# Four transformer layers on one NeuronCore: experts ordered by hand in steps of one, and sigmoid attention run inside the feed-forward's steps

## The chip, the cores and the metric

The program runs on one core of one Trainium2 chip. The core has a matrix engine (TensorE, "PE"; its weight loads are listed as "PEld"), VectorE ("DVE"), ScalarE ("ACT"), GpSimd ("POOL") and a DMA queue that SyncE ("SP") feeds. The engines run side by side, each through its own list of instructions in order, and wait for each other by semaphores. The metric is device time in microseconds; less is better.

## What is computed

A tensor x (32 x 64 x 256, here 2048 tokens of 256 values) goes through four layers of cross-attention to a context of the same shape and a feed-forward. The kernel calls the eight parts A to H. The change touches four of them:

```python
# D: causal attention with 16 heads, then four experts, two per token
a = attention(layernorm(x));  h = x_n + a                 # x_n: layernorm of x
t = layernorm(h)
raw = softmax(t @ w_gate);  top_vals, top_idx = top_k(raw, 2)
comb = scatter(softmax(top_vals), top_idx)                # (token, expert)
hmid = gelu(t @ we1[e] + be1[e]);  eout = hmid @ we2[e] + be2[e]
x = x + h + sum_e comb[:, e] * eout
# E: local attention (only its preparation is touched)
# F: two ternary products, silu(first) * second, an RMS norm, rounding, a third ternary product
x = x + linear3(silu(linear1(x_n)) * linear2(x_n))
# G: sigmoid attention of a sequence's 64 tokens; its channels play the part of positions
s = sigmoid(einsum('bdn,bdm->bnm', x_n, ctx) / 8)
x = x + einsum('bvn,bnm->bvm', ctx, s)
# H: shared and routed experts
```

## The kernel before, in words

The tokens lie in 16 tiles of 128 (xs), the context likewise (cs), and both stay in SBUF for the whole program. A stage opens pools of SBUF and PSUM tiles. Stages lie on the left and the right side of SBUF in turn, and memory of a closed pool can be used by a later one only after the last instructions on it. A stage's weights are loaded at the start of the stage before (load_D to load_H). Where no order is forced, a scheduler orders instructions for each engine; inside `tc.manual_schedule()` they stand as the program issues them. Pieces that are to lie among another stage's work are generators: each `next` issues the instructions up to the next `yield`.

**D, attention** (run_D_attention): 64 units of one head for four tiles, three units deep; a unit's steps are projections (L926, L928 to L935), scores (L941 to L953), transposes (L960), products (L970), and the sum over heads into hs (output, L985, L986).

**D, experts** (run_D_moe): four groups of four tiles. For each group in turn: norm_T normalises (ln_stats L82 to L87, ln_apply L91, transposes L97, gain and shift L521), the gate product gpl (L1038), softmax_small (L132 to L140), top2 (L115 to L127), the weights comb (to L1053) and comb's transpose (L1057). Then for each expert: hidden products hmp (L1065) with Gelu (L1068), and for each tile the output product ep (L1072), accumulated with its weight into hs on VectorE (L1075). Biases (L1079, L1080) and the sum into xs (L1081) end the group. After each expert one `next` goes to one of two generators: ternary (weights of F are read, scaled and rounded to tern, L1210 to L1226), or first_of_E (operand buffers of E are filled on VectorE, L153, and its first two tiles prepared). The scheduler orders all this.

**F** (run_F), in a hand-made order: in step t each part works on the tile t - lag. VectorE has summed (L1380), hidden (L1329), second_norm (L1348), first_sizes (xk L1284, am L1286, L1272, the factor sca L1275), second_rounding (amb L1355, hq L1358) and deviations (L1261 to L1266). ScalarE has first_copy (xT), second_copy (hT), gates (sl, Silu), squares (junk) and first_rounding (xq). GpSimd has the powers rr (L1350) and s (L1268) and gained (xr L1344). PE has the transposes xqT and hqT and the products l (L1314) and op (L1376). [...]xqT one bank, l four, hqT two, op one.

**G** (run_G), after F, groups of four tiles: normalise (L82 to L91), transpose the context (gcT L97, copied to cT on VectorE, L1409), for each of a tile's two sequences the products sp (L1415) and Sigmoid (L1419), the product gop (L1425), and the sum into xs (L1428). It lies on the left side; the weights of H (L1439 to L1447), H's table owner (L1460 to L1464) and its pools lie on the right, where F's pools lay.

**H** (run_H): routing of a group (hgp L1478), then 14 chunks of pgate and pup products (L1523), Silu (L1531), products on VectorE (L1533, L1535) and hout (L1502).

Of the kernel before, what the change touches and what calls it, by code (L numbers as in the profile page):

```python
# [17 lines left out]
P = 128  # L18
T = 2048
D = 256  # L20
# [11 lines left out]
def tile_net(ctx: ExitStack, tc: tile.TileContext, a: dict, out: bass.AP):  # L32
# [115 lines left out]
    def operand_buffers(pool, k, b):  # L148

        pair = {}  # L150
        for kind, value in (("k", 1.0), ("q", 0.0)):
            pair[kind] = pool.tile([P, 16, D], BF, name=f"st{kind}{b}")
            V.memset(pair[kind][64:P], value)  # L153
        k.setdefault("st", []).append(pair)
# [699 lines left out]
    def run_D(w, side):  # L854
        with tc.tile_pool(name="Dh", bufs=1, side=side) as hpool:
# [3 lines left out]
            hs = [hpool.tile([P, D], F32, name=f"h{i}") for i in range(NT)]  # L859
            run_D_attention(w, side, hs)  # L860
            run_D_moe(w, side, hs)

    def run_D_attention(w, side, hs):
# [4 lines left out]
        with ExitStack() as es:  # L868
# [4 lines left out]
            hnT = [tpool.tile([P, 2, 512], F32, name=f"hnT{g}") for g in range(NG)]  # L873
# [113 lines left out]

            weights_of(0)
# [19 lines left out]

    def run_D_moe(w, side, hs):
        with tc.tile_pool(name="DM2", bufs=1, side=side) as wpool, tc.tile_pool(  # L1010
            name="DMw", bufs=2, side=side
        ) as pool, tc.tile_pool(
            name="DMp", bufs=2, space=PSUM
        ) as psum:
# [4 lines left out]
            next(tern, None)  # L1019

            def others():
                for _ in range(5):
                    for gen in (first, tern):
                        next(gen, None)
                        yield
                while True:
                    for _ in range(4):
                        next(first, None)
                    yield

            other = others()
            for g in range(NG):
                ids = range(4 * g, 4 * g + 4)
                hT = norm_T(pool, psum, ids, src=hs, wb=(w["ln2_w"], w["ln2_b"]))
                gp = psum.tile([P, 4, 4], F32, tag="tp", name="gpl")
                for j in range(4):
                    for c in range(2):
                        PE.matmul(  # L1038
                            gp[:, j, :], hT[:, c, j * P : (j + 1) * P], w["gate"][:, c, :], start=c == 0, stop=c == 1
                        )  # L1040
                raw = softmax_small(pool, gp, 4, 4)
                (s1, s2), (m1, m2) = top2(pool, raw, 4, 4)
                e2 = pool.tile([P, 4], F32, name="e2")
                V.tensor_tensor(e2, m2, m1, ALU.subtract)
                S.activation(e2, e2, AF.Exp)
                w1 = pool.tile([P, 4], F32, name="w1")
                V.tensor_scalar(w1, e2, 1.0, None, ALU.add)
                V.reciprocal(w1, w1)
                V.tensor_tensor(e2, e2, w1, ALU.mult)
                V.tensor_tensor(s1, s1, bc(w1, 2, [P, 4, 4]), ALU.mult)  # L1050
                V.tensor_tensor(s2, s2, bc(e2, 2, [P, 4, 4]), ALU.mult)
                comb = pool.tile([P, 4, 4], F32, name="comb")
                V.tensor_tensor(comb, s1, s2, ALU.add)  # L1053

                tp = psum.tile([P, 4, P], F32, tag="tp", name="dcombT")
# [4 lines left out]
                for e in range(4):  # L1060
                    hm = pool.tile([P, 2, 512], F32, name="hm")
                    for ic in range(2):
                        hp_ = psum.tile([P, 512], F32, name="hmp")
                        for c in range(2):
                            PE.matmul(  # L1065
# [42 lines left out]
    def first_of_E(w, psum):  # L1108
# [4 lines left out]
        for b in range(4):  # L1113
            operand_buffers(cp, w["k"], b)
            yield
# [530 lines left out]
```

## Time and profile before

| what | value |
|---|---|
| median of the runs shown | 2878.74 us (2876.58 to 2881.87, 3 runs) |
| the profiled execution | 2879.53 us |
| its span from first to last instruction | 2877.8 us |
| busy: PE, DVE, ACT, POOL | 2468.2 (86%), 1914.5 (67%), 1531.7 (53%), 1506.4 us (52%) |
| chain that ended last, by engine | PE 50%, DVE 22%, issue 9%, POOL 5%, ACT 2%, DMA 1% |
| attention of D ends | about 1844.4 us |
| first step of F; first instruction of H's gate product | 2347.9; 2559.48 us |

The profile is of one execution. A row of the timeline has start, length, engine, line, operation, out<-in, shape and count; in brackets stands the idle time of the engine before it and what ended that. Rows of a matmul overlap, so a row of eight can be shorter than eight single ones. The chain of what ended last gives at each time the one instruction that the end waited for. A line number can be a helper's: L82 to L91 are the statistics of any stage, so the tile's name says which.

### The profile page before, as it was taken

Reading aid. Unit: us, or ns where it says so; the run is one execution under the profiler, and the core shown is the slowest. Engines: PE = TensorE matmul, PEld = TensorE weight load, DVE = VectorE, ACT = ScalarE, POOL = GpSimd, SP = SyncE. Lnnn points to the kernel's source line nnn. Section 1 sums busy time; section 2 is a strip of 40 time slices with the busy share of each in tenths; the row PEclk is TensorE's granted clock in tenths of the full one; section 3 lists DMA queues with packets and bytes.
Section 4 is the critical chain, followed back from the end, with each engine's and each line's share of the span. In section 5 each row is a group of like instructions: output and inputs, shape, how many; then the busy total and the mean of one; then the engine's idle time right before and its main releaser. Section 6 shows DMA issues by size and latency. Waiting matters only on the chain.

```text
span 2877.8 us, 44432 instructions
## 1 busy us (share of the span) xinstructions
PE 2468.2 (86%) x16072; PEld 1449.1 (50%) x16072; DVE 1914.5 (67%) x3989; ACT 1531.7 (53%) x2145; POOL 1506.4 (52%) x1681
## 2 busy tenths in 40 slices
PE   4989798777778777689999999789888976789999
PEld 2545344344444444346666666556555533445555
DVE  7877554699999999775455455663577669833332
ACT  1657221599999999655555555353345556521110
POOL 4655433588888888665555555311587754400000
PEclk9999899999999999889999999888999988999999
DMA  6553000499999999910000000001443300200000
GB/s 166 128 116 70 23 1 1 106 202 203 202 207 201 204 201 199 186 59 8 15 15 15 8 1 1 30 30 24 103 93 89 92 1 1 76 1 8 8 8 8
DMA packets 610599, 223.70 MB, mean 78 GB/s; under 512 B 547366, under 2 KB 600524, under 8 KB 605772
## 3 DMA queue, kind: packets, MB, share of 16 engines
q1 hardware_dynamic: 607308, 220.07, 35.0%
q8 instruction: 127, 2.08, 0.3%
q10 hardware_dynamic: 3072, 0.79, 0.2%
q14 instruction: 92, 0.75, 0.1%
HBM read 66.91 MB, written 18.87 MB: 30 GB/s over the span
## 4 chain that ended last, share of the span: by engine, by line
PE 50%; DVE 22%; issue 9%; POOL 5%; ACT 2%; DMA 1%; ACTq 0%; DVEq 0%; POOLq 0%; SPq 0%
DVE e L789 11%; PE yp L985 4%; PE ppq L926 3%; PE ppk L926 3%; PE hout L1502 3%; PE vp L914 3%; PE pgate L1523 3%; PE pup L1523 3%; PE sp L944 2%; PE ep L1072 2%; PE op L970 2%; PE hmp L1065 2%; PE sc L759 1%; PE op L495 1%; POOL e L286 1%
## 5 line engine op out<-in xcount | busy, mean ns | idle before, releaser
L813 ACT ACTIVATE ei<-e,nb,sq 128x2048 int16<-128x2048 f32 x256 | 535.4, 2092 | 43.4 <-DVE nb L810 39.7
L823 POOL CAST eb<-ei 128x2048 bf16<-128x2048 int16 x256 | 482.5, 1895 | 116.1 <-ACT ei L813 102.0
L759 PE MATMUL sc<-kT,qz 128*128 128x512 bf16 x1024 | 298.1, 382 | 142.0 <-DVE e L789 139.9
L246 DVE TENSOR_REDUCE negm<-s 128x2 f32<-128x512 f32 (+1 forms) x512 | 300.9, 611 | 130.6 <-PE s L242 127.4
L789 DVE TENSOR_SCALAR_CACHE_REDUCE e<-sc,mx 128x1024 f32<-128x1024 f32 x256 | 326.1, 1274 | 0.8 <-DVE nb L810 0.7
L789 DVE TENSOR_SCALAR_CACHE_REDUCE e<-sc 128x1024 f32<-128x1024 f32 x256 | 312.4, 1220 | 10.5 <-PE sc L759 10.5
L278 ACT ACTIVATE e<-s 128x1024 f32<-128x1024 f32 (+1 forms) x256 | 233.2, 915 | 152.8 <-PE s L274 117.3
L242 PE MATMUL s<-stk,stq 96*128 96x256 bf16 (+1 forms) x1024 | 192.2, 271 | 41.2 <-DMA d3k<-t3k 24.8
L759 PEld LDWEIGHTS <-qz 128*128 128x128 bf16 x1024 | 94.9, 97 | 261.2 <-issue 202.6
L934 POOL TENSOR_TENSOR rwq<-rwq,sin 128x512 f32<-128x512 f32 x64 | 81.1, 1268 | 240.1 <-ACT rwq L931 203.7
L274 PE MATMUL s<-stq,stk 128*128 128x256 bf16 (+1 forms) x1024 | 180.6, 262 | 10.8 <-DMA stq<-nm 5.4
L772 PEld LDWEIGHTS <-vz 128*64 128x64 bf16 x4096 | 123.2, 110 | 114.0 <-issue 113.9
L946 DVE TENSOR_REDUCE mx<-sp 128x4 f32<-128x512 f32 x64 | 44.3, 692 | 192.7 <-PE sp L944 192.7
L772 PE MATMUL av<-eT,vz 128*64 128x128 bf16 x4096 | 164.0, 223 | 7.3 <-DMA eT<-eb 7.2
L87 POOL TENSOR_TENSOR rstd<-ve,mhalf 128x1 f32<-128x1 f32 (+1 forms) x56 | 42.4, 757 | 240.9 <-DVE ve L85 145.9
L931 ACT ACTIVATE rwq<-ppq,dbq 64x512 f32<-64x512 f32 x128 | 87.4, 683 | 148.9 <-DVE rtq L928 148.0
L1533 DVE TENSOR_TENSOR hm<-pup,sl 128x512 f32<-128x512 f32 (+1 forms) x56 | 38.7, 692 | 191.1 <-PE pup L1523 187.4
L242 PEld LDWEIGHTS <-stq 96*128 96x128 bf16 x1024 | 93.6, 101 | 131.9 <-issue 108.6
L296 PE MATMUL o<-e,vmo 128*32 128x256 f32 (+1 forms) x2048 | 151.1, 367 | 7.4 <-POOL e L286 6.0
L1531 ACT ACTIVATE sl<-pgate 128x512 f32<-128x512 f32 (+1 forms) x56 | 33.4, 597 | 219.2 <-PE pgate L1523 219.1
L286 POOL TENSOR_SCALAR_AFFINE_SELECT e<-e 128x256 f32<-128x256 f32 (+1 forms) x256 | 133.2, 547 | 31.0 <-ACT e L278 30.3
L914 PE MATMUL vp<-Dwv,hnT 128*128 128x512 f32 x256 | 123.8, 605 | 4.0 <-ACT hnT L889 4.0
(349 smaller groups left out, 5518.5 us busy)
## 6 DMA issues: line engine op xcount, KB each, us to landing
stk<-d3k SPq DMA_DIRECT2D x96, 192.0 KB
stq<-d3q SPq DMA_DIRECT2D x96, 192.0 KB
d3k<-t3k SPq DMA_DIRECT2D x160, 64.0 KB
d3q<-t3q SPq DMA_DIRECT2D x96, 64.0 KB
eT<-eb SPq DMA_TRANSPOSE x256
fw<-in_L_ffn_w SPq DMA_DIRECT2D x3, 1024.0 KB
x<-in_x SPq DMA_DIRECT2D x16, 128.0 KB
c<-in_ctx SPq DMA_DIRECT2D x16, 128.0 KB
```

The source lines that it names most:

```text
L242: PE.matmul(sc[:, hh, lo:hi], qs[0:96, 2 * hp + hh, qc * P : (qc + 1) * P], ks[0:96, 2 * hp + hh, lo:hi], start=band is None, stop=True, s ...
L246: V.tensor_reduce(negm[:, qc, 2 * hp : 2 * hp + 2], sc[:, :, lo:hi], AX.X, ALU.max, negate=True)
L274: PE.matmul(sc[:, c, lo:hi], ks[:, h, lc * P : (lc + 1) * P], qs[:, h, lo:hi], start=True, stop=True)
L278: S.activation(e[:, :, lo:hi], sc[:, :, lo:hi], AF.Exp, scale=scale)
L759: PE.matmul(sc[:, k0 : k0 + 512], qz[i % 2][:, h, :], kT[:, h // 2, 1024 * part + k0 : 1024 * part + k0 + 512], start=True, stop=True,)
L772: PE.matmul(av[i][r0 : r0 + 64, h // 4, :], vz[:, kt, h // 4, h % 4, :], eT[:, kt, :], start=h == 0 and kt < 2, stop=h == H - 1 and kt >= ...
L789: V.tensor_scalar(e, scs.pop((n, part)), 1.0, mx[:, 0:1] if part else LOWEST, ALU.mult, ALU.max, accum_out=mx[:, part : part + 1],)
L813: S.activation(ei, es_.pop(n), AF.Exp, bias=nb, scale=sq[i][:, h : h + 1], accum_out=sums[i][:, h : h + 1],)
L823: G.tensor_copy(eb, eis.pop(n - 1))
L914: PE.matmul(vp, hnT[g][:, c, j * P : (j + 1) * P], wv[:, c, :], start=c == 0, stop=c == 1)
L926: PE.matmul(pp, wt[:, c, hh * P : (hh + 1) * P], hnT[g][:, c, :], start=c == 0, stop=c == 1)
L1523: PE.matmul(pp[:m], w[nm + "s"][:, c, cols], xnT[:, c, :], start=c == 0, stop=c == 1)
```

## The change

In **D**, routing becomes a generator, routed_D, with seven pieces. The first group's runs in attention's last steps; each later group's runs among the experts of the group before it. run_D_moe is put under manual_schedule, as 16 steps of one expert and one group: the hidden products of step n + 1 are issued ahead of the outputs of step n, and in each step up to two `next` each go to ternary, first_of_E and routing. E's operand buffers are filled on GpSimd (the new last argument). ternary has two more yields.

**F and G** are one loop of 24 steps. G's eight parts are entries of F's table with lags 5 to 7. They use F's banks (xqT, hqT0, hqT1, op); Sigmoid is written as Tanh, with a half of the context's row sums (half) as bias; normalising and the final sum are on GpSimd, the copy of the context on ScalarE. run_G returns at once. In `scales`, the factor (sca and scb) is computed by scalar_tensor_tensor with s as second tensor, not by tensor_scalar.

```diff
-    def operand_buffers(pool, k, b):
+    def operand_buffers(pool, k, b, eng=None):
...
-            V.memset(pair[kind][64:P], value)
+            (eng or V).memset(pair[kind][64:P], value)
...
+    def routed_D(w, hs, g, pool, psum, tag):
+        ids = range(4 * g, 4 * g + 4)
+        mv, rstd = ln_stats(pool, [hs[i] for i in ids])
+        yield
...
+        for j0 in (0, 2):
+            xn = []
+            for j in (j0, j0 + 1):
+                xn.append(pool.tile([P, D], F32, name="hn"))
+                ln_apply(xn[-1], hs[4 * g + j], mv, rstd, j)
+            yield
...
+            for j in range(2):
+                for c in range(2):
+                    PE.transpose(tp[:, c, j, :], xn[j][:, c * P : (c + 1) * P], ident)
+            for c in range(2):
+                S.activation(
...
+        w["routed"][g] = [hT]
+        yield
+        gp = psum.tile([P, 4, 4], F32, tag=tag, name=f"gpl_{g}", bufs=2)
+        for j in range(4):
+            for c in range(2):
+                PE.matmul(gp[:, j, :], hT[:, c, j * P : (j + 1) * P], w["gate"][:, c, :], start=c == 0, stop=c == 1)
...
+        S.activation(raw, raw, AF.Exp)
+        yield
...
+        (s1, s2), (m1, m2) = top2(pool, raw, 4, 4)
...
+        S.activation(e2, e2, AF.Exp)
+        yield
...
+        V.tensor_tensor(comb, s1, s2, ALU.add)
+        w["routed"][g].append(comb)
+        yield
...
+            ahead = routed_D(w, hs, 0, pool, psum, "vy")
...
+                if u >= NU - 3:
+                    next(ahead, None)
+            for _ in ahead:
+                pass
...
+        ) as pool, tc.tile_pool(name="DMp", bufs=2, space=PSUM) as psum, tc.manual_schedule():
...
+            def hidden(n):
+                g, e = divmod(n, 4)
+                hT = w["routed"][g][0]
+                hm = hms[n] = pool.tile([P, 2, 512], F32, name="hm")
+                for ic in range(2):
+                    hp_ = psum.tile([P, 512], F32, name="hmp")
                     for c in range(2):
                         PE.matmul(
+                            hp_, w["we1"][:, c, e, ic * P : (ic + 1) * P], hT[:, c, :], start=c == 0, stop=c == 1
                         )
+                    S.activation(hm[:, ic, :], hp_, AF.Gelu, bias=w["be1"][:, e, ic : ic + 1])
+            def output(n):
+                g, e = divmod(n, 4)
+                _, comb, combT = w["routed"][g]
+                hm = hms.pop(n)
+                for j in range(4):
+                    i = 4 * g + j
+                    ep = psum.tile([P, D], F32, name="ep")
+                    for ic in range(2):
+                        PE.matmul(
+                            ep, hm[:, ic, j * P : (j + 1) * P], w["we2"][:, e, ic, :], start=ic == 0, stop=ic == 1
+                        )
+                    V.scalar_tensor_tensor(hs[i], ep, comb[:, j, e : e + 1], hs[i], ALU.mult, ALU.add)
+                if e == 3:
+                    for j in range(4):
+                        i = 4 * g + j
+                        bp = psum.tile([P, D], F32, tag="ep", name="ebias")
+                        PE.matmul(bp, combT[:, j * P : (j + 1) * P], w["be2"], start=True, stop=True)
+                        V.tensor_tensor(hs[i], hs[i], bp, ALU.add)
+                        G.tensor_tensor(xs[i], xs[i], hs[i], ALU.add)
+            def biases(g):
+                comb = w["routed"][g][1]
+                tp = psum.tile([P, 4, P], F32, tag="hT", name=f"dcombT_{g}")
                 for j in range(4):
                     PE.transpose(tp[0:4, j, :], comb[:, j, :], ident)
                 combT = pool.tile([4, 512], F32, name="dcT", bufs=1)
                 S.copy(combT, tp[0:4].rearrange("e j t -> e (j t)"))
+                w["routed"][g].append(combT)
+            routing = iter(())
+            next(tern, None)
+            hidden(0)
+            for n in range(4 * NG):
+                g, e = divmod(n, 4)
+                if n + 1 < 4 * NG:
+                    hidden(n + 1)
+                if e == 0:
+                    biases(g)
+                    routing = routed_D(w, hs, g + 1, pool, psum, "hT") if g + 1 < NG else iter(())
+                next(first if n > 6 else tern, None)
+                if e in (1, 2, 3):
+                    next(routing, None)
+                output(n)
+                next(routing, None)
+                next(tern, None)
+                next(first, None)
...
-            operand_buffers(cp, w["k"], b)
+            operand_buffers(cp, w["k"], b, G)
...
-                V.tensor_scalar(sc, sc, s, 127.0, ALU.mult, ALU.mult)
+                V.scalar_tensor_tensor(sc, sc, 127.0, s.to_broadcast([P, n]), ALU.mult, ALU.mult)
...
+            def g_norm(i):
+                d = st[i]
+                mv, rstd = ln_stats(pool, [xs[i]], "g")
+                V.tensor_scalar(mv[:, :, 0], mv[:, :, 0], -1.0, None, ALU.mult)
+                d["q"] = pool.tile([P, D], F32, name="gq")
+                G.tensor_scalar(d["q"], xs[i], mv[:, 0, 0:1], rstd, ALU.add, ALU.mult)
...
+            def g_context(i):
+                d = st[i]
+                d["ctp"] = psum.tile([P, 2, 2, P], F32, tag="xqT", name="gcT")
+                for c in range(2):
+                    PE.transpose(d["ctp"][:, 0, c, :], cs[i][:, c * P : (c + 1) * P], ident)
+            def g_context_copy(i):
+                d = st[i]
+                d["cT"] = pool.tile([P, 2, P], F32, name="cT")
+                S.copy(d["cT"], d["ctp"][:, 0])
+
+                junk = tpool.tile([P, D], F32, name="gjunk")
+                d["half"] = pool.tile([P, 1], F32, name="half", bufs=3)
+                S.activation(junk, cs[i], AF.Identity, scale=0.5, accum_out=d["half"])
...
+            def g_scores(i):
+                d = st[i]
+                d["sp"] = []
+                for b in range(2):
+                    rows = slice(64 * b, 64 * b + 64)
+                    sp = psum.tile([P, 4, P], F32, tag=f"hqT{b}", name=f"gsp{b}").rearrange("p (n a) t -> p n (a t)", n=2)
+                    for n in range(2):
+                        PE.matmul(sp[:, n, :], d["q"][rows, n * P : (n + 1) * P], cs[i][rows, :], start=True, stop=True)
+                    d["sp"].append(sp)
...
+                for b in range(2):
+                    sg = pool.tile([P, 2, D], F32, name=f"gsg{b}")
+                    S.activation(sg, d["sp"][b], AF.Tanh, scale=0.0625)
...
+            def g_product(i):
+                d = st[i]
+                d["gop"] = psum.tile([P, D], F32, tag="op", name="gop")
+                for b in range(2):
+                    rows = slice(64 * b, 64 * b + 64)
+                    for n in range(2):
+                        PE.matmul(
+                            d["gop"][rows, :], d["cT"][:, n, rows], d["sg"][b][:, n, :], start=n == 0, stop=n == 1
+                        )
+            def g_sum(i):
+                d = st[i]
+                y = pool.tile([P, D], F32, name="gy")
+                S.activation(y, d["gop"], AF.Identity, scale=0.5, bias=d["half"])
+                G.tensor_tensor(xs[i], xs[i], y, ALU.add)
+
+            parts = [
+                (summed, 5), (first_transposes, 1), (first_copy, 1), (second_transposes, 4), (second_copy, 4),
+                (hidden, 2), (g_product, 7), (g_sum, 7), (hidden_products, 1), (gates, 1), (second_norm, 3),
+                (squares, 2), (gained, 2), (g_context, 6), (g_context_copy, 6), (first_sizes, 0), (first_rounding, 0),
+                (second_rounding, 3), (g_scores, 6), (g_tanh, 6), (output, 4), (deviations, -1), (g_norm, 5),
+            ]
-            for t in range(NT + 6):
-                for part, lag in (
-                    (summed, 5), (first_transposes, 1), (first_copy, 1), (second_transposes, 4), (second_copy, 4),
-                    (hidden, 2), (hidden_products, 1), (gates, 1), (second_norm, 3), (squares, 2), (gained, 2),
-                    (first_sizes, 0), (first_rounding, 0), (second_rounding, 3), (output, 4), (deviations, -1),
-                ):
-                    if 0 <= t - lag < NT:
+            for t in range(NT + 8):
+                for part, lag in parts:
+                    if 0 <= t - lag < NT and (with_g or not part.__name__.startswith("g_")):
...
+        if "FG" in STAGES:
+            return
```

## The prediction, made before the changed kernel ran

> **What bounds the kernel now.** I read the chain that ended last first, then cut the two stages that the change touches into stretches, then went through one step of each engine by engine in the timeline. The chain (start, length, what) at the join of attention and experts:
>
> ```profile
> 1835.81 8.22 PE yp L985 x38
> ...
> 1846.16 3.48 DVE stk L153
> ...
> 1856.16 3.47 DVE stk L153
> ...
> 1863.25 0.68 PE xnT L97 x2
> ```
>
> ```profile
> 1844.40:1863.00 18.60, 1.08 (x4) 0.71 (x4) 15.70 (x18) 1.50 (x4) 4.71 (x23) 0.57 0.17 57
> 1952.00:1990.00 38.00, 38.00 (x133) 23.14 (x132) 13.81 (x46) 12.79 (x18) 4.25 (x7) 0.91 0.00 0
> 2380.10:2471.40 91.30, 56.64 (x294) 34.00 (x295) 85.66 (x238) 55.45 (x94) 39.28 (x43) 0.89 0.00 1
> 2495.40:2559.50 64.10, 50.68 (x297) 28.46 (x297) 31.67 (x97) 20.21 (x38) 13.56 (x11) 1.00 0.29 85
> ```
>
> The columns of the stretches are length, busy time of PE, PEld, DVE, ACT, POOL, clock, DMA share, GB/s. First line: for 18.6 us after attention PE has 1.1 us of work, because VectorE fills the next stage's buffers (stk, stq) before it normalises the first experts' tokens. Second: a later group of experts is PE from end to end. Third: the feed-forward's steady steps are VectorE's (85.7 of 91.3), PE at 62% and ScalarE at 61%. Fourth: sigmoid attention is a chain of PE and ScalarE in which VectorE is half idle.
>
> In a feed-forward step VectorE repeats every 8.74 us, and GpSimd holds it up:
>
> ```profile
> 2443.78 1.32 DVE h L1329 x2
> ...
> 2452.52 1.32 DVE h L1329 x2
> ```
>
> ```profile
> 2447.45 0.99 DVE L1275 TENSOR_SCALAR sca<-sca,s 128x2 f32<-128x2 f32 x1
> ```
>
> ```profile
> 2445.93 2.49 POOL L1344 TENSOR_TENSOR xr<-h,fg 128x512 f32<-128x512 f32 x2
> ```
>
> ```profile
> 2357.99 2.46 DVE L1284 SCALAR_TENSOR_TENSOR xk<-x,mv,fg 128x256 f32<-128x256 f32 x2
> ```
>
> sca takes 0.99 us for two columns where it takes 0.23 with GpSimd quiet, and ends as xr ends. The last line is two instructions that take 0.87 together elsewhere; here xr ran from 2357.50 to 2360.18, and they waited too, though they are of the form that the change gives to sca.
>
> **Experts (-37.4 us).** From the end of attention (1844.4) to the last bias product (2033.8) are 189.4 us. PE's work at full clock, from uninterrupted pieces of the chain: hidden products 16 steps x 3.43 = 54.9; outputs 16 x 2 x 1.91 = 61.1; routing of the three remaining groups 3 x (1.88 + 4 x 0.37) = 10.1; biases 4 x (0.44 + 2.49) = 11.7; the next stage's q and k 4 x 0.43 = 1.7; three totals 1.0. Sum 140.5. The new order gives every wait a cover: the hidden products of step n+1 (3.4 us) stand ahead of the outputs of n, so PE doesn't wait for a Gelu or its table load (1.28); each routing chain is cut by yields so that its small VectorE instructions (about 0.2 each, 14 in the longest cut: 3 us) lie under those 3.4 us. Without that cover each of the three routings would cost what the old ones did: the group from 1911 to 1952 took 41.0 with 37.0 busy.
>
> What remains: the buffers' eight fills go to GpSimd. Its own fills cost 0.84 ns per bf16 column (16384 in 13.75), so 3.5 us for stk, and half that for stq, as on VectorE: some 21 us over four steps. Queued behind them on GpSimd are the tern casts and the token statistics' powers; the first powers stand ahead. While a fill runs, VectorE's normalising (of sca's kind) may wait up to 3.5 us, and behind it the accumulation that frees PE's banks; some 3 us of that is covered. Bounds 2 to 16 us of waits in all; I take 7.5, near the lower end since most covers are as long as what they cover. Stage: 148.
>
> The first group's routing moves into attention's last 11 steps. There PE is full up to 1822 and idle only 1.7 us between 1824 and 1828; it gains 1.88 + 1.48 = 3.4 us, VectorE 10 us of small work in steps of 7.6 us in which it is busy 4 to 6. Cost +1 to +6, taken as +4. Together 148 + 4 - 189.4 = -37.4. The next stage's first two tiles still go beside the experts, one or two pieces per step, with their DMAs at the end as before: nothing.
>
> **Feed-forward with sigmoid attention (-24.4 us).** From the first step (2347.9) to the last stage's gate product (2559.48) are 211.6 us.
>
> Steps 0 to 4 carry no attention: 32.2 as before (to 2380.1).
>
> Steps 5 to 15. VectorE gains four instructions (statistics 0.46, 0.21, then 0.19 and 0.15): +1.0. Rewriting sca as a product of two tensors removes nothing by the xk line: it or the small product behind it still meets xr. But xr shifts: on GpSimd it now stands behind the new sum, which waits for the step's gop, so xr runs from 3.9 to 6.4 us after the step's start and sca passes about 3.7. So the stall becomes 0 to 1.25 instead of 0.75: 9.0 to 10.25, taken as 9.6. The others fit below that. ScalarE: xq 1.08, xT 0.69, hT 1.27, sl 1.27, junk 1.25 = 5.6, plus tanh 1.09 (as sg), cT 0.37, half 0.68, gy 0.48 = 8.2. PE: 0.53 + 1.06 + 1.8 + 1.04 = 4.4, plus gop 1.57, gcT 0.37, gsp 1.13 = 7.5. GpSimd 3.7 + 0.55 + 0.56 + 0.73 = 5.5. In order, from the step's start: gop waits for summed to free their shared bank (0.45), ends 2.0; l behind it ends 3.8; sl ends 4.5, junk 5.7, cT and half 6.8, xq 7.9, tanh 9.0, the next xT 9.7, hT 10.9; the next gy is due at 9.6 + 2.05. It fits with 0.7 to spare. 11 x 9.6 = 105.6.
>
> Tail, steps 16 to 22, no longer VectorE's: op, summed, gop, gy, gcT and tanh in turn give 6.4, 5.6, 5.5, 5.1, then 11.6 us from the last summed through gop, gy of three tiles to the last sum. 34.2; with some half clock 36.
>
> Entry of the last stage: its pools lie where this stage's lay, and wait for its last instruction. Before, that was summed:
>
> ```profile
> SPq L107 <- DVE x L1380: 206.0, 1, 206.0
> ```
>
> and 5.42 MB of weights, the owner table (8.1 us before the first power) and statistics lay under 60 us of attention. Now they start at its end: fill 1.27, five selects of 1.35, power 1.03 in GpSimd's order = 9.1, then normalising 0.4 and four transposes and copies as before 3.8: 13.4 to the gate product (3.85 before). The gate weights land 7.5 us after issue by the old transfer (issue 2495.5, 335 GB/s), up 12.7, down 18.3: each just ahead of its use (about 16, 20, 32). So the load costs 0 to 5, taken as 0, its cover being the GpSimd chain; without it some 4 us.
>
> 32.2 + 105.6 + 36 + 13.4 = 187.2, against 211.6: -24.4.
>
> [...]Clock: it was 0.50 from 2434.1 to 2437.5, after 3.4 us in which PE was busy some 36% with no gap over 1.7 us; in the sigmoid stretch, 79% busy, it stayed 1.00. [...] I go by the rows: 78% busy (7.5 of 9.6) is like the sigmoid stretch, but a low 3.4 us can occur; +0 to +6. Table loads: [...] By the trace's own row (1.28 each) 10.8 and about 11.5, +21. The changed program has one load in the stage, ahead of the first Silu, and none at a tanh: I take none.
>
> **Sum.** The profiled execution took 2879.5 (span 2877.8, 1.7 around it): -37.4 - 24.4 = -61.8 gives 2817.7. The median shown is 0.8 lower: 2817.
>
> **Rivals.**
> 1. Both parts as worked out: 0.68, 2817 (2802 to 2832 with the bounds).
> 2. The fused step is worse than its sums: GpSimd's new instructions hold VectorE twice a step and half clock comes often; 11.5 a step, tail 42: +27, 2844. For: every two-tensor VectorE instruction met by xr was lengthened. Against: the h and reduce instructions that fill half of VectorE's step aren't touched. 0.16.
> 3. The experts don't become PE's: fills and casts hold VectorE through the first group, and comb holds the bias transposes; 165 instead of 148, 2834. Against: the later groups already ran at 38 of 38. 0.10.
> 4. Slower: PE at half clock through the fused stage. 7.5 becomes 15.0, plus the 0.5 wait for summed 15.5 a step; tail 50: +65 +14 = 2896. It decides from a mean step of 15.2 (61.8 / 11 above 9.6). For: 0.62 mean clock in the stage's first 32 us. Against: 1.00 over the whole sigmoid stretch. 0.03.
> 5. The change doesn't do what it says: steps stay apart or tanh reloads tables. The order built shows them joined. 0.03, about 2839.
>
> Slower sum: 0.03. A measurement tells about 0.2% (6 us) from no change; within that 0.02; faster 0.95. Range 2798 to 2843: it takes in rival 3, most of 2, and the low bounds.
>
> **What would show it.** PE idle under 3 us between attention and experts, PE over 90% busy from there to the end of the experts, and some 150 us for them: the experts' step. VectorE periods of 9 to 10.3 us between the h instructions, DVE still the fullest engine: the fused step. No table load at tanh. sca short but the following small product or xk long: the stall moved. The last sum to the gate product 12 to 15 us, ended by GpSimd's power. It would be wrong if PE's clock falls in the fused steps, if PE waits for banks in the experts, or if weights end the wait at the last stage.

## The result, and the profile after

| | before | after |
|---|---|---|
| median (4 runs each) | 2879.16 us (2876.58 to 2881.87) | 2836.48 us (2829.32 to 2839.6) |
| ratio after to before | | 0.9848, 95% interval 0.9826 to 0.9870 |
| profiled execution; its span | 2879.53; 2877.8 us | 2838.68; 2837.0 us |
| attention's last sum to the experts' last bias product | 189.3 us | 169.3 us |
| of it PE idle | 28.7 us | 22.4 us |
| from there to the feed-forward's first step (stage E) | 314.1 us | 318.0 us |
| from there to the last stage's gate product (F and G) | 211.6 us | 184.8 us |
| from there to the end (H) | 318.3 us | 318.5 us |

The change made the kernel 1.5% faster. The fusion gave 26.8 us, more than the 24.4 predicted. The experts gave 20.0 instead of 41.4, and stage E, which the change was not to touch, took 3.9 back.

The chain of what ended last, at the join of attention and experts. Before, two fills of VectorE stood here:

```profile
1845.92 0.43 DVE h L1043
...
1846.40 2.00 PE hmp L1091 x4
...
1862.17 7.28 DVE hn L91 x2
...
1874.10 4.59 DVE hn L91 x2
1878.69 2.20 DVE wpart L1271
...
1892.92 5.32 DMA fw<-in_L_ffn_w
1898.26 2.29 DVE wpart L1271
...
1903.86 3.78 PE ep L1104 x8
```

PE now starts 0.05 us after attention's last sum. But the end then waits for VectorE's normalising (hn), for the reduction of the ternary weights (wpart), and for these weights' DMA. The same normalising took, in the kernel before (named xn there):

```profile
1859.67 0.75 DVE xn L91 x2
```

The stretches, with columns as in the prediction (length, busy time of PE, PEld, DVE, ACT, POOL, clock, DMA share, GB/s):

```profile
1863.00:1910.20 47.20, 29.07 (x95) 19.65 (x93) 25.41 (x42) 12.61 (x17) 25.56 (x12) 0.75 0.13 45
1951.70:1987.60 35.90, 35.90 (x137) 23.01 (x138) 18.43 (x61) 14.18 (x21) 8.58 (x16) 0.95 0.19 48
2394.22:2459.64 65.42, 49.92 (x322) 29.08 (x322) 61.39 (x176) 50.29 (x105) 38.96 (x50) 1.00 0.00 1
2503.85:2518.49 14.64, 2.75 (x8) 1.16 (x9) 10.44 (x36) 1.52 (x5) 11.39 (x9) 0.55 1.00 283
```

First line: most of the first group; PE has work for 29.1 of 47.2 us, at a clock of 0.75. Second: the third group is PE from end to end, as predicted for all. Third: seven fused steps; VectorE is full (61.4 of 65.4), the clock 1.00. Fourth: the entry of the last stage.

One fused step, in the timeline:

```profile
2412.82 1.40 DVE L1394 SCALAR_TENSOR_TENSOR h<-l,dqa,sl 128x512 f32<-128x512 f32 x2
...
2416.14 2.50 POOL L1409 TENSOR_TENSOR xr<-h,fg 128x512 f32<-128x512 f32 x2
...
2416.49 0.93 DVE L1340 SCALAR_TENSOR_TENSOR sca<-sca,s 128x2 f32<-128x2 f32 x1
...
2422.17 0.74 DVE L1394 SCALAR_TENSOR_TENSOR h<-l,dqa,sl 128x512 f32<-128x512 f32 x1
```

The period is 9.35 us (2412.82 to 2422.17). sca still takes 0.93: it ends at 2417.42, when the first of xr's two instructions (1.25 each) ends.

And the start of stage E, first in the kernel before, where the first statistics followed the last bias sum (it ends at 2034.26) by 0.04 us, then in the changed kernel:

```profile
2034.30 0.43 DVE L82 BATCH_NORM_STATS2 bnst<-x 128x6 f32<-128x256 f32 x1
```

```profile
2021.05 0.43 DVE L82 BATCH_NORM_STATS2 bnst<-x 128x6 f32<-128x256 f32 x1 [3.81 <-DMA d3q<-t3q]
```

They are now 4.95 us behind it (2016.10). For the last 3.81 of these VectorE waited for the write of tile 1's q (d3q<-t3q).

### The profile page after: what moved, and what is told of

Read it like the earlier page. It is cut to its first block, busy times and chain, and to the rows that moved or that the text cites. A ratio compares the mean times of both kernels' runs of the same rounds, so it can differ in the third digit from the quotient of the medians.

```text
span 2837.0 us, 44436 instructions
## 1 busy us (share of the span) xinstructions
PE 2441.6 (86%) x16072; PEld 1437.3 (51%) x16072; DVE 1892.7 (67%) x3961; ACT 1531.6 (54%) x2186; POOL 1560.0 (55%) x1733
## 4 chain that ended last, share of the span: by engine, by line
PE 48%; DVE 22%; issue 9%; POOL 7%; ACT 2%; DMA 1%; ACTq 0%; DVEq 0%; POOLq 0%; SPq 0%
DVE e L789 11%; PE yp L1042 4%; PE ppq L983 4%; PE ppk L983 4%; PE hout L1628 3%; PE vp L971 3%; PE pgate L1649 3%; PE pup L1649 3%; POOL e L286 2%; PE ep L1104 2%; PE sp L1001 2%; PE op L1027 2%; PE hmp L1091 2%; PE sc L759 1%; PE op L495 1%
## 5 line engine op out<-in xcount | busy, mean ns | idle before, releaser
L813 ACT ACTIVATE ei<-e,nb,sq 128x2048 int16<-128x2048 f32 x256 | 535.4, 2092 | 44.4 <-DVE nb L810 40.8
L242 PE MATMUL s<-stk,stq 96*128 96x256 bf16 (+1 forms) x1024 | 191.5, 270 | 40.9 <-DMA d3k<-t3k 24.4
```

The source lines that it names most:

```text
L242: PE.matmul(sc[:, hh, lo:hi], qs[0:96, 2 * hp + hh, qc * P : (qc + 1) * P], ks[0:96, 2 * hp + hh, lo:hi], start=band is None, stop=True, s ...
L813: S.activation(ei, es_.pop(n), AF.Exp, bias=nb, scale=sq[i][:, h : h + 1], accum_out=sums[i][:, h : h + 1],)
```

## The experiments

My theory after the two traces: the missing time lies in three waits of VectorE in the first expert group, one behind another, each with the accumulations that free PE's banks queued behind it (PE's ep waits 18.6 us for h in the first two groups), and in E's late start. The rivals: one cause covers the others, so that removing one brings nothing; or the two parts of the change disturb each other; or PE's clock is a cause of its own. The stages of all runs, cut as in the table above (us, one profiled execution each; the ratio is to the kernel before):

| run | experts | PE idle in them | E | F and G | ratio of times, with 95% interval |
|---|---|---|---|---|---|
| before | 189.3 | 28.7 | 314.1 | 211.6 | |
| after | 169.3 | 22.4 | 318.0 | 184.8 | 0.9848 (0.9826 to 0.9870) |
| d_only | 167.6 | 21.4 | 317.5 | 211.0 | 0.9950 (0.9935 to 0.9966) |
| fg_only | 189.2 | 28.6 | 313.9 | 184.8 | 0.9901 (0.9883 to 0.9919) |
| fills_small | 156.6 | 15.4 | 317.5 | 183.9 | 0.9821 (0.9799 to 0.9844) |
| fw_two | 156.6 | 14.8 | 317.5 | 185.4 | 0.9820 (0.9806 to 0.9835) |
| fills_vector | 167.6 | 21.9 | 317.7 | 185.1 | 0.9849 (0.9827 to 0.9871) |
| first_early | 167.5 | 21.4 | 318.5 | 183.7 | 0.9842 (0.9822 to 0.9861) |
| h_left | 167.5 | 21.4 | 318.4 | 189.6 | 0.9878 (0.9859 to 0.9898) |
| h_weights | 167.5 | 21.5 | 317.8 | 181.6 | 0.9841 (0.9821 to 0.9861) |
| sca_ts | 167.5 | 21.5 | 318.4 | 184.5 | 0.9853 (0.9833 to 0.9873) |
| xr_small | 167.6 | 21.4 | 317.5 | 175.8 | 0.9820 (0.9803 to 0.9838) |
| best_s | 143.2 | 5.2 | 315.5 | 179.7 | 0.9749 (0.9732 to 0.9765) |
| best_sx | 142.0 | 2.9 | 315.1 | 173.5 | 0.9715 (0.9698 to 0.9733) |

H is 318.1 to 319.3 in all. Attention's end varies from 1840.8 to 1848.2 us with no relation to the edits, so a difference of a few us in the total is read from the stages.

**Each part alone** (d_only: F and G apart; fg_only: D as before).

```diff
-        with_g = "FG" in STAGES
+        with_g = False
...
     def run_G(w, side):
-        if "FG" in STAGES:
-            return
```

> The experts' part of the change alone: steps of one expert, routing ahead, fills on GpSimd; feed-forward and sigmoid attention stay two stages, and sca keeps the rewritten form. By the theory from the two traces (attention +1.9, experts 189.4 to 169.3, next stage +4.0 because its first statistics wait for the write of tile 1's q) this gives -14 us, about 2865, and the same 169 us between attention's last sum and the last bias product. If the two parts help or hurt each other (the rival), it is off by more than 4 us.

> The fusion alone: feed-forward and sigmoid attention in common steps, experts as before. By the stretches of the changed trace (feed-forward's first step to the last stage's gate product 211.6 to 184.8) -27 us, about 2852, with VectorE periods of 9.35 us. Together with the experts' part alone the two should sum to -41. Rival, that the fusion is worth what was left over only because the stage before ended differently: off by more than 4 us.

Measured: 2862.75 and 2848.34 against 2876.08 before, -13.3 and -27.7 us. The sum, -41.0, is what both gave together (-42.7 by the medians, -40.8 by the spans). The parts don't touch each other, so that rival falls; the miss is all in the first.

**Fills in pieces.**

```diff
-            (eng or V).memset(pair[kind][64:P], value)
+            for h in range(8):
+                (eng or V).memset(pair[kind][64:P, 2 * h : 2 * h + 2], value)
```

> The changed kernel with each of the eight fills cut in eight (512 columns, about 0.45 us each), in the same places on GpSimd. Theory, a running GpSimd fill holds VectorE's normalising to its end and so the accumulations that free PE's banks: the two hn pairs go from 7.28 and 4.59 us to under 2 each, PE's gaps of 6.4 and 3.3 us in the first group to under 1.5 each, some half clock goes with them: -7 to -11 us, the first group 64 to 54 or so. Rival, PE waits there for the ternary weights' reduction and would wait as long without the fills: 0 to -2, the gaps stay.

In the changed kernel's timeline the normalising and the fills beside it:

```profile
1862.17 7.28 DVE L91 TENSOR_SCALAR hn<-h,mv,rstd 128x256 f32<-128x256 f32 x2 [0.74 <-POOL rstd L87]
1862.19 3.51 POOL L153 MEMSET stk<- 64x4096 bf16 x1
1865.64 3.65 POOL L153 MEMSET stq<- 64x4096 bf16 x1
```

and the same rows with the fills in pieces:

```profile
1861.90 1.30 DVE L91 TENSOR_SCALAR hn<-h,mv,rstd 128x256 f32<-128x256 f32 x2 [0.74 <-POOL rstd L87]
1861.93 4.07 POOL L154 MEMSET stk<- 64x512 bf16 x8
```

The same fill takes 0.56 us more in all, and the two hn take 1.30 instead of 7.28: here the two were held by pieces of some 0.5 us (4.07 for eight) and no longer to the ends of whole fills. PE's gaps of 6.4 and 3.3 us shrink to nothing and 1.9. Experts 156.6 us, 12.7 less than in the changed kernel's profile and 10.9 less than the 167.5 of the runs that leave this stage alone: at or above the upper end of the 7 to 11 expected, though the second gap stayed above the 1.5 expected. Some 6 to 7 of it is idle time, the rest clock (below).

**Two buffers for the raw weights.**

```diff
-                raw = tpool.tile([P, 2048], F32, name="fw")
+                raw = tpool.tile([P, 2048], F32, name="fw", bufs=2)
```

> The changed kernel with two buffers for the feed-forward's raw weights, so that the third block loads while the second is still read. Theory, VectorE's third reduction waits 5.3 us for that block with the accumulations queued behind it: the 8.4 us gap of PE in the first group falls to 2 to 3 (the reduction, 2.3, and 14 small routing instructions, 2.7, still stand ahead, with 3.4 of hidden products as cover): -5 to -7 us. Rival, fills set the first group and the block would be waited for elsewhere: 0 to -2.

What PE waited for from attention's end to the end of the second group (us in total, times, longest), in the changed kernel and with two buffers:

```profile
PE ep L1104 <- DVE h L1107: 18.6, 3, 8.4
PE wtot L1274 <- DVE wpart L1271: 3.3, 1, 3.3
```

```profile
PE ep L1104 <- DVE h L1107: 11.6, 3, 6.4
PE wtot L1274 <- DVE wpart L1271: 2.8, 1, 2.8
```

The third gap falls from 8.45 to 1.43 us, the fills' gap of 6.4 stays. Two separate causes, then, each worth 6 to 8 us of idle time; neither covers the other. The rival that one sets the group falls. The stage got 10.9 to 12.7 us shorter here too, more than the 5 to 7 expected.

The surplus is clock: in both runs PE's work in this stage took some 5 us less as well (141.2 and 141.8 for 146.9). The first group in the changed kernel and with small fills, the same instructions of PE:

```profile
1846.40:1910.20 63.80, 45.28 (x146) 28.88 (x146) 33.01 (x59) 18.86 (x25) 27.39 (x13) 0.81 0.15 50
```

```profile
1846.10:1897.40 51.30, 40.12 (x145) 24.79 (x145) 23.64 (x58) 18.86 (x25) 29.35 (x55) 0.90 0.19 62
```

With less idle time the clock of this group was 0.90 instead of 0.81, in fw_two as well, and its matmuls took 5.2 us less (2.9 in fw_two). So most of the low clock came and went with the gaps. But the rival of a clock with a cause of its own is not settled: in the changed kernel it fell to 0.50 at 1911.4 and at 1952.3, for 3.4 us each, behind 3.4 us in which PE was busy for 3.36 and 3.40.

**Fills on VectorE again.**

```diff
-            operand_buffers(cp, w["k"], b, G)
+            operand_buffers(cp, w["k"], b)
```

> The changed kernel with the eight fills back on VectorE, one pair per expert step as now. Theory: a fill then stands in VectorE's own queue (3.5 and 1.8 us), ahead of accumulations, with 3.4 us of hidden products as cover: four waits of PE of some 2 to 3 us each instead of 6.4 and 3.3; the hn pairs 0.8 us each. Experts 167 to 170, so 0 to +3 us against the changed kernel. Rival, moving them to GpSimd was what made the experts' stage PE's: +10 us or more.

167.6 us, as expected, and as with the fills on GpSimd (167.5 to 169.3). PE's waits:

```profile
PE ep L1104 <- DVE h L1107: 21.5, 4, 8.5
```

Moving the fills to GpSimd brought nothing: PE waited 21.5 us in all with the fills on VectorE and 21.9 (18.6 + 3.3 above) with them on GpSimd. Of this the fills' own gaps are 5.7 and 3.6 on VectorE, 6.4 and 3.3 on GpSimd; the gaps of 8.5 and 3.7 behind the weights' DMA and the ternary scales are the same in both. The rival falls: what made the later groups PE's is the order, the only other change to this stage.

**E's first tiles earlier.**

```diff
                 next(first if n > 6 else tern, None)
+                if n > 10:
+                    next(first, None)
```

> The changed kernel with the next stage's first two tiles taken one piece more per step in the last five expert steps, so that tile 1's q is written before the experts end and not after. Theory, the next stage's first statistics lie where tile 1's staging buffers lay and wait for their write to DRAM (4.95 us behind the last bias sum, 0.04 before the change): the stretch from the experts' last bias product to the feed-forward goes from 318.0 back to 314: -4 to -5 us. Rival, GpSimd's token sums and the casts behind them set that start whatever the pieces do: 0 to -1, and the experts' last group gets longer by what was moved into it.

Half right. The wait for the write is gone:

```profile
2009.82 0.43 DVE L82 BATCH_NORM_STATS2 bnst<-x 128x6 f32<-128x256 f32 x1 [1.02 <-POOL x L1114]
```

The first statistics stand 1.02 us behind the last bias sum instead of 4.95, and what they still wait for, 1.02 us, is GpSimd's token sum, which is what the rival named. But of these 3.9 us only 2.6 arrive at the end of E's first tile: it ends 74.7 us after the last bias product, against 77.3 in the changed kernel and 73.4 before. On the chain in between, one DMA (stq<-nm) took 6.12 us instead of 5.05; why it did is open. Later tiles of the changed kernel keep an offset of 3.4 to 4.0 to the kernel before. E as a whole was no shorter in this profile (318.5): later tiles lost 1.8 and some 1.4 us that no other run shows, and that I can't name. The time can't tell 4 us from none. In the two combined runs, which hold the same edit, the first tile ended at 74.7 and 74.3 and E took 315.5 and 315.1. So the wait for tile 1's write was all 3.9 us at E's start, and taking it away gave back 2.6 to 3.

**Last stage on the other side of the memory** (h_left, the first cut), or only its weights and table (h_weights, which has both cuts and builds the table where the weights are loaded).

```diff
-STAGES = "ABCDEFGH"
+STAGES = "ABCDEFH"
...
-        with_g = "FG" in STAGES
+        with_g = True
```

```diff
-        runs[s](cur[1], cur[2])
+        runs[s](cur[1], "right" if s == "H" else cur[2])
...
-            owner = cp.tile([96, 1408], BF, name="owner")
...
+            owner = w["owner"]
```

> The changed kernel with the last stage on the other side of the memory (its weights and buffers free since the end of the attention before the feed-forward), and nothing else moved by hand; the scheduler then puts the owner table before the feed-forward's first steps and the last stage's token statistics among its later ones. Theory, the 14.6 us between the last sum and the gate product are the price of sharing the feed-forward's memory, GpSimd's table (9.1) the longest part: they fall to 4 to 5 (four transposes and copies), -10 us, less what the statistics cost VectorE in the fused steps (16 tiles x 0.67 = 10.7 us, up to half of it in steps that VectorE sets: +0 to +5). Together -5 to -10. Rival, the weights' 5.42 MB set the entry: then it also falls, but the weights' landing is seen in no wait; rival two, the powers and transposes set it: -2 at most.

> As the run before, but only the weights and the owner table go to the other side; statistics and working buffers stay where the feed-forward's lay. So the entry keeps statistics (2.5 us), power (1.03), normalising and four transposes and copies (3.8): some 8 us instead of 14.6, -6.5, with nothing added to the fused steps; the table's 9.4 us on GpSimd now stand among the powers of the feed-forward's first two steps and may cost 0 to 5 there. If the weights and not the table set the entry, the same -6.5; if neither, 0.

The entry of the last stage fell as expected: 14.6 us in the changed kernel, 3.1 in h_left, 8.6 in h_weights. In both the price came elsewhere. h_left is slower: the scheduler put the last stage's statistics into VectorE's queue within the fused steps, where they wait for the sums and powers of GpSimd with the steps' own work behind them, and most periods went from 9.35 us to between 10.6 and 12.9:

```profile
2417.64 0.43 DVE L82 BATCH_NORM_STATS2 bnst<-x 128x6 f32<-128x256 f32 x1 [1.30 <-POOL x L1503]
...
2421.58 0.41 DVE L91 TENSOR_SCALAR xn<-x,mv,rstd 128x256 f32<-128x256 f32 x1 [2.01 <-POOL rstd L87]
```

I had counted their 0.67 us of work a tile and not these waits. In h_weights GpSimd builds the table beside the feed-forward's first steps, ahead of a power (s) that VectorE needs:

```profile
2337.07 1.45 POOL L1579 TENSOR_SCALAR_AFFINE_SELECT owner<-owner 32x1408 bf16<-32x1408 bf16 x1
2338.60 0.56 POOL L1333 TENSOR_TENSOR s<-ve,mhalf 128x1 f32<-128x1 f32 x1
2339.19 1.42 DVE L1337 TENSOR_SCALAR am<-am,s 128x2 f32<-128x2 f32 x1 [1.17 <-POOL s L1333]
```

The first h came 11.6 us after the stage's start instead of 8.5, and the gain of 6.0 shrank to 3.2.

**sca in its old form.**

```diff
-                V.scalar_tensor_tensor(sc, sc, 127.0, s.to_broadcast([P, n]), ALU.mult, ALU.mult)
+                V.tensor_scalar(sc, sc, s, 127.0, ALU.mult, ALU.mult)
```

> The changed kernel with sca's last product in its old form (one tensor, one per-partition scalar, a constant) instead of two tensors. Theory (as in the prediction): both forms wait for the GpSimd product that runs, sca stays at 0.9 to 1.0 us in the fused steps and the period at 9.35: 0, within 2 us. Rival, the rewrite [...]is worth its 0.7 us a step: +7 to +11 us.

As expected: sca 0.94 to 1.28 in the steps that meet xr, most periods 9.40, F and G 184.5. The rival falls. The rewrite is worth 0.05 us a step, its shorter time when nothing holds it (0.16 against 0.23).

**xr in eight pieces.**

```diff
-                for nh in range(2):
-                    ns = slice(nh * 512, (nh + 1) * 512)
-                    G.tensor_tensor(d["xr"][:, ns], d["h"][:, nh, :], w["g3"][:, ns], ALU.mult)
+                hf = d["h"].rearrange("p a n -> p (a n)")
+                for nh in range(8):
+                    ns = slice(nh * 128, (nh + 1) * 128)
+                    G.tensor_tensor(d["xr"][:, ns], hf[:, ns], w["g3"][:, ns], ALU.mult)
```

> The changed kernel with GpSimd's gain product xr in eight pieces of 128 columns instead of two of 512. Theory, sca waits to the end of the GpSimd instruction that runs, not of all the work queued: sca falls from 0.98 to 1.06 us to under 0.6 and the period of the fused steps from 9.35 to 8.8 to 9.0: -4 to -7 us over the stage. Rival, [...]the pieces lengthen xr so that the next VectorE instructions (dqa, amb, hq) are met in sca's place: period 9.3 or more, 0 or slower.

```profile
2416.34 3.79 POOL L1410 TENSOR_TENSOR xr<-h,fg 128x128 f32<-128x128 f32 x8
2416.57 0.24 DVE L1340 SCALAR_TENSOR_TENSOR sca<-sca,s 128x2 f32<-128x2 f32 x1
...
2421.86 1.40 DVE L1394 SCALAR_TENSOR_TENSOR h<-l,dqa,sl 128x512 f32<-128x512 f32 x2
...
2430.70 1.40 DVE L1394 SCALAR_TENSOR_TENSOR h<-l,dqa,sl 128x512 f32<-128x512 f32 x2
```

xr as a whole grew from 2.50 to 3.8, and still sca fell to 0.24 and most periods to 8.84. sca ended at 2416.81, 3.3 us ahead of the end of xr's last piece, so it did not wait for all of GpSimd's queued work, and the period is under the rival's 9.3: the rival falls. F and G took 175.8, 9.0 less than in the changed kernel and more than the 4 to 7 expected: 4.9 in the eleven fused steps, and 1.6 in the five steps ahead of them and 2.5 in the tail, which I had not counted.

**Together.** best_s holds the small fills, the two buffers, the earlier tiles, one more yield in front of the last two instructions of the ternary scales (they had kept PE waiting 3.7 us in the second group), the last stage's weights on the other side and its table as one select per step of the tail; best_sx has xr in pieces as well.

```diff
             S.activation(a2, sw, AF.Ln, bias=1.0, scale=-1.0)
+            yield
             V.tensor_tensor(at, at, a2, ALU.subtract)
...
                         part(t - lag)
+                if t == NT - 1:
+                    G.memset(shared["owner"], 1.0)
+                if NT <= t < NT + 6:
+                    rows = shared["owner"][32 * ((t - NT) // 2) : 32 * ((t - NT) // 2) + 32]
+                    sg, base = ((1, 0), (-1, 175))[(t - NT) % 2]
+                    G.affine_select(rows, rows, [[sg, 1408]], ALU.is_ge, 0.0, base=base, channel_multiplier=-176 * sg)
```

> Together: fills in pieces, two buffers for the raw weights, first tiles taken earlier, the last piece of the ternary scales one call later, the last stage's weights on the other side of the memory and its owner table spread over six steps of the feed-forward's tail. Sum of the parts as the runs showed them: fills 9.6 of PE's waits, weights 7, scales 2 to 3, clock in their gaps 5 to 6, so experts from 167.5 to about 145; next stage's first tile -2.6; entry of the last stage 14.6 to 8 (-6.5), nothing added to the fused steps: -30, about 0.974 of the kernel before. If the waits hide one another (rival: the next late thing is the routing's own chain in front of the accumulations), experts stay at 152 or more and the sum at -22.

> The run before with xr in eight pieces as well: its own gain on top, -4 to -7 us more if sca's wait is by the instruction; else no better.

Measured 2806.23 and 2795.27 us against 2878.64 before: the second takes 2.85% less time than the kernel before, and by the two ratios 1.35% less than the changed one (0.9715 / 0.9848). Its experts, group one, two and the last two:

```profile
1842.60:1885.70 43.10, 40.24 (x145) 24.83 (x145) 24.80 (x59) 18.86 (x25) 28.06 (x53) 0.94 0.21 74
1885.70:1922.20 36.50, 36.42 (x138) 23.14 (x137) 20.30 (x65) 18.18 (x25) 18.93 (x48) 0.93 0.00 0
1922.20:1984.60 62.40, 62.39 (x241) 40.70 (x241) 30.26 (x90) 20.65 (x31) 16.20 (x28) 1.00 0.23 55
```

142.0 us with 2.9 idle, so 139.1 of work. So the waits were the named ones (the scales' yield was not run alone), and PE's own sum of 140.5 in the prediction was sound. The clock in these lines is 0.94, 0.93 and 1.00: one stretch of 10.2 us at half clock was left (1880.3 to 1890.5), 1 us behind a gap of 2.0. The entry fell to 8.6 us. But the fused stage's last sum came 1.0 us later in best_s than in the changed kernel, counted from the stage's start, and 3.7 later in best_sx than in xr_small; 0.6 and 3.7 of it are in the tail. The selects were added there. That they are the cause is not shown: scb, on VectorE, took 2.0 us twice in best_s's tail instead of 0.77, but no more than 0.43 in best_sx's, which lost more.

## Why the prediction was right or wrong

The forecast was 2817, in a range of 2798 to 2843; it came to 2836.5. Direction and range hold, the likeliest case doesn't: its two parts were -37.4 and -24.4, and the profile shows -14.2 and -26.8. The range held because it took in rival 3, to which I gave 0.10; in the case that I had at 0.68 the experts' half failed.

**Experts, -37.4: wrong, in the waits, taken as 7.5 us and as the fills' alone, and in PE at full clock.** PE was idle 22.4 us, above my upper end of 16, and its work took 146.9 instead of 140.5. Four gaps make up nearly all of the 22.4: 6.4 and 3.3 behind the fills, 8.45 behind the weights' DMA and 3.7 behind the scales. So the fills' own part, 9.6, came near the 7.5; what failed is that the other two were put at nothing. By the runs:

1. "While a fill runs, VectorE's normalising ... may wait up to 3.5 us": right for one hn, but two fills stood back to back and each pair of hn met both, 7.28 for the first pair. That the sum still came near is partly luck, since the other four fills met no hn. I also gave stq half of stk's time on GpSimd, as on VectorE. It took 3.51 to 3.65. VectorE's row of before is a uint32 of half the elements (64x2048, 1.77 us, beside 3.47 for stk), GpSimd's of after a bf16 of 64x4096. The half was my estimate from VectorE's rows, and GpSimd's own didn't show it: its zero fill of before from which I took the 0.84 ns is bf16 (128x16384 in 13.75). All eight fills came to 28.4 us, not 21. The pieces (fills_small) gave back 7.0 us of idle time.
2. The ternary weights: I counted their totals on PE and GpSimd's casts, but not that in the new order the reduction, which waited 7.70 us for a DMA into the one buffer, stands ahead of accumulations in VectorE's list. 8.45 us in one gap, 7.0 of it given back by a second buffer. This is the step that asks what is queued behind a waiting instruction; I asked it of the fills alone. The scales' last instructions cost 3.7 in the second group in the same way: VectorE was idle for 7.88 us until ScalarE's logarithms (watanh) were there, with accumulations behind it.
3. "PE's work at full clock": in the first group the clock was 0.81, and the same instructions took some 5 us more than with small fills. The idle time above the 7.5 (14.9 us) and the slower matmuls (6.4) make up the 21.3 us between 148 and 169.3: best_sx, without most of both, took 142.0.

"since most covers are as long as what they cover" was the error behind these: 3.4 us of hidden products cover one wait, not three in a row.

**"with their DMAs at the end as before: nothing": wrong, +3.9.** The last piece of tile 1 is now issued after the last expert step, its casts stand behind the token sums on GpSimd, and E's first statistics wait for its write (3.81 us). The three runs that take it earlier give back 2.6 to 3 us of it.

**Attention +4:** its end came 1.9 later in this pair, but attention took 626.3 to 630.2 us in all runs, with and without routing in it (626.3 and 629.4 without). Within what I said, and not resolved.

**Fused stage, -24.4: right, -26.8, with each stretch near its sum:** the first five steps 32.1 (32.2), eleven fused steps 102.2 (105.6: 9.35 each in the middle and 8.41 at the end, for 9.6), tail 35.9 (36), entry 14.6 (13.4). The entry ended as written:

```profile
2508.08 2.75 POOL L1590 TENSOR_SCALAR_AFFINE_SELECT owner<-owner 32x1408 bf16<-32x1408 bf16 x2
2510.88 1.35 POOL L1589 TENSOR_SCALAR_AFFINE_SELECT owner<-owner 32x1408 bf16<-32x1408 bf16 x1
2512.32 1.02 POOL L87 TENSOR_TENSOR rstd<-ve,mhalf 128x4 f32<-128x4 f32 x1
```

The selects end, then the power, for which normalising waits 3.59 us; the 5.42 MB of weights landed beside it and ended no wait ahead of the gate product. "Rewriting sca ... removes nothing" was right. "sca passes about 3.7" was wrong: it began 3.7 us after h did, but xr had begun at 3.3 (2416.14 against 2412.82) and not at 3.9, so the stall stayed in sca, about 0.9 us of it where the 9.6 has room for 0.6. That the step still came out shorter than 9.6 is luck: the four instructions that I added at 1.0 us were in part there before. Eight of the old steps already held a tile's statistics for sigmoid attention, as the scheduler had placed them (line L82 with x, 0.42 us, and L83, 0.17):

```profile
2445.86 0.42 DVE L82 BATCH_NORM_STATS2 bnst<-x 128x6 f32<-128x256 f32 x1
```

**The clock and the table loads.** The clock was 1.00 in the fused steps, with PE busy 76% and no pause of it over 1 us in the steady ones, as in the sigmoid stretch to which I compared them (1.00, 79%). The one low stretch that I argued from is a reading to set right: PE was busy 36% of the four us from 2430 to 2434, but 45% (1.52 of 3.40) in the 3.4 us just ahead of the drop. There was no table load at a tanh, and one of 1.28 us in the stage, at 2338.68; the 10.8 us of ScalarE and the +21 were for two such loads a step.

**GpSimd's fills and VectorE.** In numbers: hn 7.28 beside whole fills and 1.30 beside pieces; wpart 2.29 beside a fill (1898.26) and 2.29 with GpSimd idle (1851.40). One wait of some 3.5 us per fill that an hn meets is what was seen; I had that size from the rows, and counted too few meetings.

**The rivals.** Rival 3, at 0.10, had part of the mechanism and nearly the number: fills hold VectorE through the first group, 165 us and 2834, measured 169.3 and 2836.5. It doesn't name the weights' DMA or the scales. Its second half, bias transposes waiting for comb, did not occur. Rivals 2, 4 and 5 did not occur.

## What to carry to other kernels

When an order is fixed by hand, list for each instruction that can wait (for a DMA, for a long instruction of another engine, for another engine's result) what stands behind it on its engine, and add the waits of one group: a cover counts once. Try long instructions that only prepare something, such as fills, in pieces where the trace shows another engine's instructions held up by them: here eight pieces took 4.07 us instead of 3.51, and the experts came out 10.9 to 12.7 us shorter. A stage that begins early in its own memory may move its work into the queue of the engine that is full, as in h_left, where most periods went from 9.35 us to between 10.6 and 12.9; ask whose queue the scheduler will use.

## What the runs showed that I had not expected

- In the changed kernel two of VectorE's 128x256 tensor_scalar (hn) met two of GpSimd's fills of 64 partitions (3.51 and 3.65 us) back to back and took 7.28 us for the two, to the end of the second fill; two of the same shape (xn) took 0.75 in the kernel before.
- The gaps and a low clock went together: cutting the fills' gaps from 9.6 us (6.38 and 3.26) to 1.9 came with 5 us less for the same matmuls of that group, at a granted clock of 0.90 instead of 0.81.
- Cutting GpSimd's product into eight made it 1.3 us longer (2.50 to 3.79) and the whole step 0.5 us shorter (9.35 to 8.84).
